# A message-passing layer on one core: the position and flag steps of a block in other iterations, and the variance chain first in its GpSimd queue

## The chip, the cores and the metric

One core of one Trainium2 chip runs the whole layer in one launch. The metric is the time of that launch on the device, in microseconds (us). Engines are named as the profile names them: PE (matmul) and PEld (its weight loads), DVE (VectorE), ACT (ScalarE), POOL (GpSimd), SP (SyncE, which issues the DMAs).

## The reference, cut to what matters

128 graphs of 64 nodes, 128 channels, a 0/1 adjacency with a full diagonal. Each edge gets a message from a three-layer MLP with two layer norms; the messages are summed per node, and a second MLP updates the node.

```python
pair_feats = concatenate([f_i, f_j], axis=-1)          # x of the two ends of each pair
messages = _mlp(pair_feats, msg_w0, msg_b0, ...)       # relu, layernorm, relu, layernorm, linear
messages = messages * coupling_matrix[..., None]       # adj: only edges count
agg = sum(messages, axis=2)
updated = x + _mlp(concatenate([x, agg]), upd_w0, upd_b0, ...)

def _layernorm(x, g, b):
    mu = mean(x); var = mean(square(x - mu))
    return (x - mu) * rsqrt(var + EPS) * g + b
```

## The kernel before, in words

The kernel computes messages for real edges only. The edges of a graph are packed into 640 places, five tiles of 128. Two graphs make a pair `p`, two pairs a quad `q` (20 tiles), and eight graphs (four pairs, two quads) a block `b`. There are 16 blocks, 32 quads, and 160 chunks of four tiles.

**Positions.** For a block, `rank` (DVE scan), `count` (PE), `count_out` and `degrees` (ACT) count edges. `place` (POOL, lines 379, 381, 383) turns the counts into `before`, `mid` and `pos`. `place_out` (line 392, two instructions) masks the positions into `posall`, and `odd_marks` (lines 415, 416) makes `a2`, from which `odd_weights` (DVE) later raises a flag. `distance` (ACT, line 467, tile `d`) reads `mid`; `make_tp` (DVE) makes `tp` from it; `marks` (PE, line 495, tile `mk`) reads `posall` and `tp`. From these come the selectors `s` for layer 0.

**The edge MLP.** One iteration `n` of the main loop handles chunk `n` in layer 0 and chunk `n - 8` in layer 1: `layer1` (PE line 567 and 570 into `z`, ACT line 573 to `y`), `layer0` (PE line 521 into `hps`, ACT line 524 to `h`), `stats0` (PE transposes line 530 into `hT`, DVE line 534 to `st`), `stats1` (DVE line 580 on `y`). PSUM tiles `z`, `hps`, `hT` and `mk` have one buffer each.

**The variance chain.** After the fifth chunk of a quad, `var0_of` (POOL, five small instructions, lines 247 to 251, tile `m`) makes the variance from `st`. In the next iteration `root_of` takes the root on ACT (line 257, `m_sd`), copies it rounded on ACT (line 548), and takes the rest on POOL (line 549, tile `sh`). `turn_root` transposes `sh` on PE (line 554, into `ma`), and ACT copies it to `sdT` (line 559), which layer 1 of that quad reads.

**Other POOL work.** `weights` (line 636, tile `w`, two instructions a pair) scales the one-hot matrices; `var1_step` repeats the variance chain for layer norm 2 (tile `m_v`); per block the node update has `bias0` (lines 683, 686, tile `m`), `residual` (line 690, tile `xo`), `upd_shift` (line 731, tile `usdb`) and two small chains (tile `um`). `reduce` (PE line 651, tile `ys`) sums messages with `w`; `rows` (PE lines 442, 444) makes the next layer-0 tables.

**What sets the order.** The order is written out by hand. `at(n, place, fn, ...)` enters a call into iteration `n` at a place of it; the loop runs the places in a fixed order, and each engine executes its own instructions strictly in that order, waiting on semaphores for others:

```python
run(n, "a"); run(n, "m"); layer1(n - L1); run(n, "b"); layer0(n)
stats0(n - 1); run(n, "k"); stats1(n - L1)
for k in ("x", "x1", "x2", "e1", "e"): run(n, k)
```

Block `b` starts with layer 0 at iteration `o = 10 * b`; quad `q` has its `var0_of` in iteration `5 * q + 5`, entered at "e1", and its `root_of` and `turn_root` one iteration later. `weights` is also at "e1", in iterations 5q + 15 and 5q + 16, and is entered ahead of `var0_of`; nearly all other POOL work is at "e". Below, "iteration 0" to "iteration 9" of a block's period means `n` modulo 10. An odd quad has `var0_of` in iteration 0 and `turn_root` in iteration 1, an even quad in iterations 5 and 6.

Of the kernel before, what the change touches and what calls it, by code (L numbers as in the profile page):

```python
# [23 lines left out]
def tile_gnn(  # L24
# [262 lines left out]
    def edge_path(es):  # L287
# [35 lines left out]
        def at(n, place, fn, *args):  # L323
            plan.setdefault((n, place), []).append((fn, args))

        def run(n, place):
            for fn, args in plan.pop((n, place), ()):
                fn(*args)
# [186 lines left out]
        def layer0(n):  # L515

            ps = ps_h.tile([P, CH * P], F32, name="hps")
            for g, e, c, w in pieces(n):
                s = S[g // 2][:, g % 2, e:e + w]
                for k, ab in enumerate(blocks[g // (2 * PB)]["ab", g // 4 % 2]):  # L520
                    nc.tensor.matmul(ps[:, c:c + w], lhsT=ab[:, g % 4, :], rhs=s,  # L521
                                     start=(k == 0), stop=(k == 1))
            H[n] = hp.tile([P, CH * P], F32, name="h")
            nc.scalar.activation(H[n], ps, AF.Relu, bias=b0c)  # L524

        def stats0(n):
            q, c = divmod(n, QC)
            ps = ps_t.tile([P, CH, P], F32, name="hT")
            for t in range(CH):
                nc.tensor.transpose(ps[:, t, :], H[n][:, t * P:(t + 1) * P], ident)  # L530
            if c == 0:
                ST0[q] = stp.tile([P, QT, 6], F32, name="st0", bufs=2)
            for t in range(CH):
                nc.vector.bn_stats(ST0[q][:, CH * c + t, :], ps[:, t, :])  # L534
# [27 lines left out]
        def layer1(n):  # L562

            q, c = divmod(n, QC)
            ps = ps_z.tile([P, CH, C], F32, name="z")
            h = H.pop(n)
            nc.tensor.matmul(ps, lhsT=SD[q], rhs=W["b1t"][:, CH * c:CH * c + CH, :], start=True,  # L567
                             stop=False, skip_group_check=True)
            for t in range(CH):
                nc.tensor.matmul(ps[:, t, :], lhsT=h[:, t * P:(t + 1) * P], rhs=W["w1c"],  # L570
                                 start=False, stop=True, skip_group_check=True)
            Y[n] = yp.tile([P, CH, C], F32, name="y")
            nc.scalar.activation(Y[n], ps, AF.Relu)  # L573

        def stats1(n):
            q, c = divmod(n, QC)
            if c == 0:
                ST1[q] = stp.tile([P, QT, 6], F32, name="st1", bufs=2)
            for t in range(CH):
                nc.vector.bn_stats(ST1[q][:, CH * c + t, :], Y[n][:, t, :])  # L580
# [122 lines left out]
        def layer(u, *pairs):  # L703
            ps = u.bank()
            for q in range(u.n):
                s = slice(q * P, (q + 1) * P)
                for n, (src, w) in enumerate(pairs):
                    l = (u.blk["xnT"][:, (u.k0 + q) * P:(u.k0 + q + 1) * P] if src == "xn" else
                         getattr(u, src)[:, s])
                    nc.tensor.matmul(ps[:, s], lhsT=l, rhs=w, start=(n == 0),  # L710
                                     stop=(n == len(pairs) - 1))
            u.l_ps = ps[:, 0:u.n * P].rearrange("p (q c) -> p q c", q=u.n)
# [50 lines left out]
        for b in range(NB):  # L763
            o = b * CPB
            if b > 1:
                at(max(o - 25, 0), "a", load_adj, b)
                at(max(o - 12, 0), "a", load_x, b)
            if b > 0:
                r = max(o - 13, 1)
                at(max(o - 14, 0), "m", rank, b)  # L770
                at(r, "x", count, b)
                at(r + 1, "a", count_out, b)
                at(r + 1, "a", degrees, b)
                at(max(o - 11, r + 1), "e", place, b)
                at(max(o - 10, r + 2), "e", place_out, b)
                at(max(o - 10, r + 2), "e", odd_marks, b)
                at(o - 4, "m", odd_weights, b)
                at(o - 3, "x", turn_x, b)
                at(o - 2, "a", turn_x_out, b)
            for half, n in ((0, o - 2), (1, o + 3)):  # L780
                if n >= 0:
                    at(n, "x2", rows, b, half)
                    at(n + 1, "a", rows_hi, b, half)
                    at(n + 1, "m", rows_lo, b, half)

            if b < NB - 2:
                units = [(Unit(b, 0, PB, nc.gpsimd, ubank), o + QC + SC, STEADY)]
            elif b == NB - 2:
                units = [(Unit(b, 0, PB, nc.gpsimd, ubank), o + QC + SC, LAST[0])]
            else:  # L790
                units = [(Unit(b, 0, 2, nc.gpsimd, hbank), o + SC, LAST[1]),
                         (Unit(b, 2, 2, nc.vector, zbank), o + QC + SC - 3, LAST[2])]
            for u, n, t in units:
                at(n - 2, "e", bias0, u)
                at(n + t[0], "a", sums_out, u)
                at(n + t[1], "x", turn, u, "ysum")
                at(n + t[2], "a", turn_out, u, "ysum")
                at(n + t[3], "x", lambda u: layer(u, ("xn", u0a), ("ysumT", W["w2u"])), u)
                at(n + t[4], "m", layer_out, u, "uh", "m0")
                at(n + t[4], "e", upd_m0, u)  # L800
                at(n + t[5], "x", turn, u, "uh")
                at(n + t[6], "a", turn_out, u, "uh")
                at(n + t[7], "a", upd_root0, u)
                at(n + t[7], "e", upd_shift, u)
                at(n + t[8], "x", lambda u: layer(u, ("uhT", W["u1c"])), u)
                at(n + t[8], "e", residual, u)
                at(n + t[9], "m", layer_out, u, "uy", "usdb")
                at(n + t[9], "e", upd_m1, u)
                at(n + t[10], "x", turn, u, "uy")
                at(n + t[11], "a", turn_out, u, "uy")  # L810
                at(n + t[12], "a", upd_root1, u)
                at(n + t[12], "m", upd_inverse, u)
                at(n + t[13], "x", lambda u: layer(u, ("uyT", W["u2c"])), u)
                at(n + t[14], "m", finish, u)
        for p in range(NP):
            n = p * TG * 2 // CH
# [13 lines left out]
            at(NCHK + L1 + 2 if last else p // 2 * QC + SC, "x1", reduce, p)  # L830
        for q in range(NQ):
            n = q * QC + QC
            at(n, "e1", var0_of, q)
            at(n + 1, "b", root_of, q)
            at(n + 1, "x", turn_root, q)
            at(n + 2, "a", root_out, q)
            at(n + L1, "e1", var1_step, q)
            at(n + L1 + (1 if q == NQ - 1 else 2), "a", root1_of, q)
            at(n + L1 + (1 if q == NQ - 1 else 2), "m", inverse_of, q)
# [100 lines left out]
        for n in range(last + 1):  # L940
            run(n, "a")
            run(n, "m")
            if 0 <= n - L1 < NCHK:
                layer1(n - L1)
            run(n, "b")
            if n < NCHK:
                layer0(n)
            if 0 <= n - 1 < NCHK:
                stats0(n - 1)
            run(n, "k")  # L950
            if 0 <= n - L1 < NCHK:
                stats1(n - L1)
            for k in ("x", "x1", "x2", "e1", "e"):
                run(n, k)

        return flag
# [1 line left out]
    with ExitStack() as es:  # L958
        es.enter_context(tc.manual_schedule())
        flag = edge_path(es)  # L960
# [160 lines left out]
```

## Time and profile before

| | us |
|---|---|
| median of 3 runs (lowest, highest) | 650.14 (649.91, 653.18) |
| profiled execution | 653.32 |
| its span, first to last instruction | 651.5 |
| PE busy | 587.4 (90%) |
| DVE busy | 460.8 (71%) |
| ACT busy | 382.5 (59%) |
| POOL busy | 356.4 (55%) |

The span is 1.8 us shorter than the time of its execution. The share of busy time is an average over the span; which engine sets the pace in the loop is read from who waits for whom. A matmul in the profile is pipelined with its neighbours, so that a busy PE is one without gaps. The mean clock granted to TensorE was 0.967 of full speed.

### The profile page before, as it was taken

To read this page: it belongs to the slowest core of one execution; us is meant where nothing else is said; L and a number is where in the kernel's file an instruction comes from. 1 tells how busy PE (TensorE), PEld (TensorE's weight loads), DVE (VectorE), ACT (ScalarE), POOL (GpSimd) and SP (SyncE) were. 2 spreads that over 40 slices of the span, in tenths; PEclk is the share of its full clock that TensorE was granted. 3 is DMA by queue.
4 is the path that set the end of the run, shared out by engine and by line. 5 is a ranking of instruction groups with operands and counts; after the bars stand their busy time and mean duration, and the time that the engine had idled before them with its cause. 6 is when DMAs were issued, how large, how long until landed. Compare 5 with 4: busy or idle time off the path is not lost. (4 is left out here: it accounts for less than half of the span.)

```text
span 651.5 us, 15485 instructions
## 1 busy us (share of the span) xinstructions
PE 587.4 (90%) x5393; PEld 542.0 (83%) x5393; DVE 460.8 (71%) x1868; ACT 382.5 (59%) x781; POOL 356.4 (55%) x919
## 2 busy tenths in 40 slices
PE   5889989898998989899898989999898989998875
PEld 4668879797997979799798979889797979998764
DVE  6666648687676777677687868757786876785674
ACT  5765646665665667475556756655566666663422
POOL 2732355745647574654757465564856556364652
PEclk8998989899999999999999999989999998999998
DMA  4553545345354534625353463444444343431101
GB/s 121 137 139 70 113 93 114 78 112 109 84 127 97 119 88 116 124 64 135 91 130 84 114 122 82 114 108 116 101 114 102 98 104 87 105 95 38 23 17 35
DMA packets 91085, 63.84 MB, mean 98 GB/s; under 512 B 57462, under 2 KB 74876, under 8 KB 91004
## 3 DMA queue, kind: packets, MB, share of 16 engines
q1 hardware_dynamic: 90716, 62.69, 41.3%
q8 instruction: 44, 0.72, 0.5%
q14 instruction: 37, 0.30, 0.1%
q10 hardware_dynamic: 288, 0.13, 0.1%
HBM read 6.82 MB, written 4.19 MB: 17 GB/s over the span
## 5 line engine op out<-in xcount | busy, mean ns | idle before, releaser
L534 DVE BATCH_NORM_STATS2 st<-hT 128x6 f32<-128x128 f32 x640 | 142.3, 285 | 106.8 <-PE hT L530 106.3
L570 PEld LDWEIGHTS z<-w1c,h 128*128 128x128 f32 x1280 | 173.9, 197 | 7.2
L570 PE MATMUL z<-w1c,h 128*128 128x128 f32 x1280 | 174.1, 280 | 0.0
L636 POOL TENSOR_TENSOR w<-oh,m_q 128x320 f32<-128x320 f16 x124 | 86.9, 722 | 152.7 <-PE mk L495 138.2
L573 ACT ACTIVATE y<-z 128x512 f32<-128x512 f32 x160 | 95.5, 597 | 92.1 <-PE z L570 92.1
L580 DVE BATCH_NORM_STATS2 st<-y 128x6 f32<-128x128 f32 x640 | 137.6, 277 | 4.9 <-ACT y L573 4.9
L524 ACT ACTIVATE h<-hps,b0c 128x512 f32<-128x512 f32 x160 | 109.5, 685 | 3.8 <-PE hps L521 3.8
L530 PE MATMUL hT<-ident,h 128*128 128x128 f32 x640 | 98.8, 278 | 0.0
L521 PE MATMUL hps<-s,abl 128*128 128x512 f32 (+3 forms) x256 | 94.6, 380 | 0.4 <-ACT h L524 0.4
L530 PEld LDWEIGHTS hT<-ident,h 128*128 128x128 f32 x640 | 77.7, 143 | 10.0 <-DVE st L534 0.3
L567 PE MATMUL z<-b1t,sdT 80*128 80x512 f32 x160 | 80.5, 503 | 1.6 <-ACT y L573 1.6
L521 PE MATMUL hps<-s,abh 128*128 128x512 f32 (+3 forms) x256 | 80.5, 332 | 0.0
L651 PE MATMUL ys<-y,w 128*64 128x128 f32 x1280 | 78.2, 278 | 0.0
L651 PEld LDWEIGHTS ys<-y,w 128*64 128x64 f32 x1280 | 70.5, 139 | 7.3 <-issue 7.0
L503 DVE TENSOR_TENSOR j<-mk,cmpt 128x320 fp32r<-128x320 f32 x126 | 59.7, 473 | 1.5 <-PE mk L495 1.4
L458 DVE TENSOR_TENSOR abl<-mu,abh 128x512 fp32r<-128x512 f32 x32 | 22.1, 690 | 50.2 <-ACT abh L451 50.2
L467 ACT ACTIVATE d<-slot,mid 128x640 f16<-128x640 f16 x64 | 53.4, 834 | 0.0
L521 PEld LDWEIGHTS hps<-s,abl 128*128 128x128 f32 x256 | 51.4, 201 | 1.7 <-ACT i L479 0.8
L521 PEld LDWEIGHTS hps<-s,abh 128*128 128x128 f32 x256 | 51.4, 201 | 0.0
L451 ACT CAST abh<-mu 128x512 fp32r<-128x512 f32 x32 | 18.7, 585 | 48.3 <-PE mu L444 48.3
L479 ACT CAST i<-tp 128x640 fp32r<-128x640 f16 x63 | 45.4, 720 | 1.9 <-DVE tp L473 1.9
L554 PE MATMUL ma<-ident,sh 128*80 128x128 f32 x32 | 10.0, 312 | 38.2 <-POOL sh L549 38.1
(221 smaller groups left out, 1000.1 us busy)
## 6 DMA issues: line engine op xcount, KB each, us to landing
s<-i SPq DMA_DIRECT2D x126, 160.0 KB, 2.7
s<-j SPq DMA_DIRECT2D x126, 160.0 KB, 2.6
xn<-in_x_dram SPq DMA_DIRECT2D x15, 256.0 KB, 3.8
out_dram<-uo SPq DMA_DIRECT2D x15, 256.0 KB, 2.4
an<-in_adj_dram SPq DMA_DIRECT2D x16, 128.0 KB, 2.7
oh<-tp SPq DMA_TRANSPOSE x64, 2.6
xn<-in_x_dram SPq DMA_DIRECT2D x2, 128.0 KB
out_dram<-uo SPq DMA_DIRECT2D x2, 128.0 KB
```

The source lines that it names most:

```text
L467: nc.scalar.activation(D[p], slot, AF.Abs, bias=blocks[b]["mid"][:, q:q + 1], scale=-1.0)
L503: nc.vector.tensor_tensor(JR[p][:, c], MK.pop((p, k))[:, 0:HC], cmpt[:, c], op=ALU.is_equal)
L521: nc.tensor.matmul(ps[:, c:c + w], lhsT=ab[:, g % 4, :], rhs=s, start=(k == 0), stop=(k == 1))
L524: nc.scalar.activation(H[n], ps, AF.Relu, bias=b0c)
L530: nc.tensor.transpose(ps[:, t, :], H[n][:, t * P:(t + 1) * P], ident)
L534: nc.vector.bn_stats(ST0[q][:, CH * c + t, :], ps[:, t, :])
L567: nc.tensor.matmul(ps, lhsT=SD[q], rhs=W["b1t"][:, CH * c:CH * c + CH, :], start=True, stop=False, skip_group_check=True)
L570: nc.tensor.matmul(ps[:, t, :], lhsT=h[:, t * P:(t + 1) * P], rhs=W["w1c"], start=False, stop=True, skip_group_check=True)
L573: nc.scalar.activation(Y[n], ps, AF.Relu)
L580: nc.vector.bn_stats(ST1[q][:, CH * c + t, :], Y[n][:, t, :])
L636: (nc.vector if p // 2 == NQ - 1 else nc.gpsimd).tensor_tensor(w[:, :, g, :], OH[p][:, :, g * N:(g + 1) * N], Q[q][:, k:k + TG].unsqueeze( ...
L651: nc.tensor.matmul(YS[b][g * N:(g + 1) * N, k, :], lhsT=w[:, t, g, :], rhs=y, start=(t == 0), stop=(t == TG - 1))
```

## The change

Two edits. In every block from the third on (`b` = 2 to 15), `place` moves from iteration `o - 11` to `o - 9`, and `place_out` with `odd_marks` from `o - 10` to `o - 7`, all still at place "e", behind whatever that iteration has entered before. And `var0_of` gets a place "e0" of its own, run ahead of "e1", so that it stands ahead of `weights`.

```diff
-                at(max(o - 11, r + 1), "e", place, b)
-                at(max(o - 10, r + 2), "e", place_out, b)
-                at(max(o - 10, r + 2), "e", odd_marks, b)
+                at(max(o - 9, r + 1), "e", place, b)
+                at(max(o - 7, r + 2), "e", place_out, b)
+                at(max(o - 7, r + 2), "e", odd_marks, b)
...
-            at(n, "e1", var0_of, q)
+            at(n, "e0", var0_of, q)
...
-            for k in ("x", "x1", "x2", "e1", "e"):
+            for k in ("x", "x1", "x2", "e0", "e1", "e"):
```

No instruction is added or removed. Only POOL's queue changes its order: PE, DVE, ACT and SP have the same rows in the same order as before, with other buffer numbers. On POOL there are three places, shown for one period in the middle of the program.

POOL before, from iteration 9 to iteration 1 of a period (odd quad): the last two rows of `place`, then `weights`, the five variance instructions, `place_out`, `odd_marks`, and only then `sh`.

```order
L381 TENSOR_TENSOR mid<-cumall,before 128x4
L383 TENSOR_TENSOR pos<-rk,before 128x256
L636 TENSOR_TENSOR w<-oh,m_q 128x5x64 x2
L247 TENSOR_TENSOR m_d<-st_4047 128x20
L248 TENSOR_TENSOR m_s<-st_4047 128x20
L249 TENSOR_TENSOR m_d<-m_d 128x20
L250 TENSOR_SCALAR m_d<-m_d 128x20
L251 TENSOR_TENSOR m_4325<-m_d,m_s 128x20
L392 TENSOR_TENSOR posall<-pos,an 64x4x64 x2
L415 TENSOR_TENSOR a_4333<-an 128x256
L416 TENSOR_TENSOR a_4333<-a_4333,an 128x256
L549 TENSOR_TENSOR sh<-m_sd,sh 128x40
```

Of these rows, the first two and those of lines 392 to 416 move to later iterations, and the `w` pair moves behind line 251.

POOL after, iterations 0 and 1 of the same period: the variance instructions first, then `weights` of the first pair, then `sh`; behind `sh` the second pair's `weights`, `residual`, `bias0`, and now `place`.

```order
L247 TENSOR_TENSOR m_d<-st_4047 128x20
L248 TENSOR_TENSOR m_s<-st_4047 128x20
L249 TENSOR_TENSOR m_d<-m_d 128x20
L250 TENSOR_SCALAR m_d<-m_d 128x20
L251 TENSOR_TENSOR m_4316<-m_d,m_s 128x20
L636 TENSOR_TENSOR w<-oh,m_q 128x5x64 x2
L549 TENSOR_TENSOR sh<-m_sd,sh 128x40
L636 TENSOR_TENSOR w<-oh,m_q 128x5x64 x2
L690 TENSOR_TENSOR xo<-xn,cu2b 128x512
L683 TENSOR_TENSOR m_4381<-c2u,deg 128x512
L686 TENSOR_TENSOR m_4381<-m_4381,ub0b 128x512
L379 TENSOR_TENSOR before<-cumall,deg 128x4
```

So four instructions left the stretch between `m` and `sh`, one pair of `w` entered it, and `place` went from an idle stretch to the end of iteration 1's queue.

POOL after, iteration 3 to iteration 5 of that period: `place_out` and `odd_marks` now follow the layer norm 2 chain (`m_v`), ahead of the even quad's variance chain. Before, line 265 was followed there by `w`.

```order
L265 TENSOR_TENSOR m_v<-m_v,m_4516 128x20
L392 TENSOR_TENSOR posall<-pos,an 64x4x64 x2
L415 TENSOR_TENSOR a_4525<-an 128x256
L416 TENSOR_TENSOR a_4525<-a_4525,an 128x256
L247 TENSOR_TENSOR m_d<-st_4357 128x20
```

What moved there: the two steps that stood ahead of `sh` stand two iterations behind it.

## The prediction

> **What bounds the kernel now.** I read the page first, then the list of who waits for whom, then the order of time around the largest wait. From the page: the span, TensorE's busy share, and the granted clock in 40 slices. From the list of waits, TensorE's two largest.
>
> ```profile
> span 651.5 us, 15485 instructions
> PE 587.4 (90%) x5393; PEld 542.0 (83%) x5393; DVE 460.8 (71%) x1868; ACT 382.5 (59%) x781; POOL 356.4 (55%) x919
> PEclk8998989899999999999999999989999998999998
> ...
> PE ma L554 <- POOL sh L549: 38.1, 17, 3.3
> PE mk L495 <- DVE tp L473: 4.9, 3, 3.5
> ```
>
> PE is idle for 651.5 - 587.4 = 64.1 us, and 38.1 us of that is one wait: the transpose of `sh` (line 554) for POOL. It occurs 17 times. The next wait is an eighth of it. Three of the 17 stand outside the places that the change touches; these are their rows in order of time.
>
> ```profile
> 30.33 0.31 PE L554 MATMUL ma<-ident,sh 128*80 128x128 f32 x1 [1.87 <-POOL sh L549]
> ...
> 65.86 0.31 PE L554 MATMUL ma<-ident,sh 128*80 128x128 f32 x1 [0.34 <-POOL sh L549]
> ...
> 607.80 0.31 PE L554 MATMUL ma<-ident,sh 128*80 128x128 f32 x1 [0.98 <-POOL sh L549]
> ```
>
> The other 14 hold 38.1 - 1.87 - 0.34 - 0.98 = 34.9 us. They are the odd quads of blocks 2 to 15, one per block; no even quad of the steady loop is in the list. Here is one of them in order of time (start, duration, engine, line; in brackets the idle time before it and what ended it).
>
> ```profile
> 381.63 0.89 DVE L534 BATCH_NORM_STATS2 st<-hT 128x6 f32<-128x128 f32 x4
> 381.81 1.40 POOL L636 TENSOR_TENSOR w<-oh,m_q 128x320 f32<-128x320 f16 x2 [5.29 <-PE mk L495]
> 383.17 0.25 POOL L247 TENSOR_TENSOR m_d<-st 128x20 f32<-128x20 f32 x1
> 384.22 0.23 POOL L251 TENSOR_TENSOR m<-m_d,m_s 128x20 f32<-128x20 f32 x1
> 384.40 1.52 POOL L392 TENSOR_TENSOR posall<-pos,an 64x256 f16<-64x256 f32 x2
> 384.48 0.31 ACT L257 ACTIVATE m_sd<-m,eps_c 128x20 f32<-128x20 f32 x1 [0.54 <-POOL m L251]
> 384.82 0.23 ACT L548 CAST sh<-m_sd 128x40 fp32r<-128x40 f32 x1
> 386.00 0.61 POOL L415 TENSOR_TENSOR a<-an 128x256 f32<-128x256 f32 x1
> 386.69 0.72 POOL L416 TENSOR_TENSOR a<-a,an 128x256 f32<-128x256 f32 x1
> 387.38 0.27 POOL L549 TENSOR_TENSOR sh<-m_sd,sh 128x40 fp32r<-128x40 f32 x1
> 387.70 0.31 PE L554 MATMUL ma<-ident,sh 128*80 128x128 f32 x1 [2.35 <-POOL sh L549]
> ```
>
> ACT has delivered the rounded root at 384.82 + 0.23 = 385.05, but POOL is in `place_out` and `odd_marks` until 387.41. PE has been ready since 387.70 - 2.35 = 385.35. A second loss ahead of it: the statistics are complete at 381.63 + 0.89 = 382.52, and the chain starts at 383.17, when `w` is done.
>
> **The stall also costs clock.** The first two rows are whole periods of a block between two such transposes, the others stretches right at or after one (columns: stretch, its length, busy time by engine, granted clock, DMA).
>
> ```profile
> 387.70:424.70 37.00, 34.66 (x334) 32.49 (x334) 27.83 (x114) 23.28 (x47) 21.98 (x58) 1.00 0.44 108
> 424.70:463.30 38.60, 36.24 (x334) 34.01 (x334) 27.72 (x114) 23.38 (x47) 21.97 (x58) 0.96 0.42 103
> ...
> 45.90:52.70 6.80, 5.94 (x24) 4.92 (x24) 0.92 (x4) 2.59 (x6) 1.06 (x3) 0.50 0.50 121
> 537.40:540.60 3.20, 3.19 (x14) 3.10 (x15) 0.28 (x2) 0.85 (x2) 3.20 (x4) 0.50 0.88 197
> ```
>
> A full-clock period has 37.00 - 34.66 = 2.34 us of PE idle time, which is the stall and nothing else: PE sets the pace, and every microsecond of the stall that goes shortens the span. After seven of the 14 stalls the clock is at half for some 3.4 us (after the first, at 46.76, for 6.8 us; those two rows are the first and the last of the seven). Such a period lasts 38.60 instead of 37.00 us. In the PEclk line five of the seven drops show as an 8 (two are split between slices); the first and the last 8 are the program's ends.
>
> **The change, part by part.** *Variance chain first.* Between engines a hand-over takes about 0.05 (`sh` ends at 387.38 + 0.27 = 387.65, PE starts at 387.70); I allow 0.08, so POOL can start `m_d` at 382.60 instead of 383.17. The five instructions take 384.45 - 383.17 = 1.28, so `m` is ready at 383.88. ACT then delivers its copy within the 0.60 it now needs (385.05 - 384.45), at about 384.5.
>
> *place_out and odd_marks out.* They held 387.41 - 384.40 = 3.0 us between `m` and `sh`. The pair `w` with 1.40 takes their place: from 383.84 to 385.24. Its inputs were there at 381.81, 2 us earlier, so it does not wait. `sh` starts at 385.20 instead of 387.38, and PE at 385.52 instead of 387.70. **Gain 2.18 us**, with 0.17 of stall left. Times 14: 30.5 us. The bounds are 34.9 (all of the stall) and, if `w` ran 0.5 slower in its new place, 23.5. I take 30.5, since the durations are those of the same instructions.
>
> *Even quads.* There `sh` now stands behind `w`: 1.40 behind `m` instead of some 0.6, with `m` 0.57 earlier; 0.2 us later in all. No even quad has PE waiting, and the nearest bound is the odd quad's 0.17 left over: 0, at worst 14 x 0.2 = 3.
>
> *place moved behind the queue of iteration 1.* Before, it ran in POOL's idle time in iteration 9; the rows of its duration come first. Now it follows `sh`, `w`, `xo` and `m` (`bias0`), and ACT's `d` in iteration 3 needs its `mid`. All these rows are of before:
>
> ```profile
> 375.48 0.20 POOL L379 TENSOR_TENSOR before<-cumall,deg 128x4 f32<-128x4 f32 x1
> 375.75 0.20 POOL L381 TENSOR_TENSOR mid<-cumall,before 128x4 f32<-128x4 f32 x1
> ...
> 387.61 1.40 POOL L636 TENSOR_TENSOR w<-oh,m_q 128x320 f32<-128x320 f16 x2
> 388.96 1.29 POOL L690 TENSOR_TENSOR xo<-xn,cu2b 128x512 f32<-128x512 f32 x1
> 390.21 1.04 POOL L683 TENSOR_TENSOR m<-c2u,deg 128x512 f32<-128x512 f32 x1
> 390.23 0.83 ACT L467 ACTIVATE d<-slot,mid 128x640 f16<-128x640 f16 x1
> 391.33 1.28 POOL L686 TENSOR_TENSOR m<-m,ub0b 128x512 f32<-128x512 f32 x1
> 391.33 0.60 ACT L573 ACTIVATE y<-z 128x512 f32<-128x512 f32 x1 [0.28 <-PE z L570]
> 391.87 0.69 ACT L524 ACTIVATE h<-hps,b0c 128x512 f32<-128x512 f32 x1
> 392.35 2.40 PE L651 MATMUL ys<-y,w 128*64 128x128 f32 x40
> 392.69 0.22 POOL L263 TENSOR_SCALAR um_v<-um 128x4 f32<-128x4 f32 x1
> 395.56 0.50 PE L567 MATMUL z<-b1t,sdT 80*128 80x512 f32 x1
> 395.94 0.23 POOL L265 TENSOR_TENSOR m_v<-m_v,m 128x20 f32<-128x20 f32 x1
> 396.71 0.48 PE L521 MATMUL hps<-s,abl 128*128 128x512 f32 x1
> ```
>
> In these rows' clock (subtract 2.18 for the new one): `m` ends at 392.61, so `mid` is ready at 392.69 + 0.47 = 393.16, while `d` would start at 390.23. ACT waits 2.9 us, in twelve blocks (4 to 15; in block 3, where `xo` is missing, 1.3 us less). Behind `d` in ACT's queue stand `y` and `h` of iteration 3; they end at 393.2 + 0.83 + 0.60 + 0.6 = 394.6 for `y` and 395.3 for `h`. Who needs them? PE's next `z` needs the bank that `y` reads, but PE is first in `reduce` (2.40 us) and `rows`, and comes to `z` at 395.56: 0.9 later. Its next `hps` is at 396.71: 1.4 after `h`. So the wait is covered by `reduce` and `rows`; cost 0, and up to 2.9 x 12 + 1.6 = 36 us if the cover were gone.
>
> *place_out two iterations later.* POOL's small chains (`um` and `m_v`) run from 392.69 to 396.17, now some 1.1 later because of `place` ahead: to 397.3. `place_out` ends at 398.8, `odd_marks` at 400.2. Their readers, still in that clock:
>
> ```profile
> 399.79 0.30 PE L495 MATMUL mk<-tp,posall 128*128 128x320 f16 x1
> 399.99 0.89 DVE L534 BATCH_NORM_STATS2 st<-hT 128x6 f32<-128x128 f32 x4
> ```
>
> `mk` reads `posall` 1.0 us after it is written, and the even quad's statistics are complete at 400.88, 0.7 after POOL comes free. Cost 0, with thin margins: each microsecond of POOL beyond them would show as 14 us.
>
> *Clock.* If the stalls go, so should the drops. Seven drops, eight stretches of 3.4 us (the first counts twice), each worth 38.60 - 37.00 = 1.6 us: 12.8. Bounds 0, and 8 x 3.4 / 2 = 13.6. I take 12.8, because no full-clock period in the trace shows a drop elsewhere.
>
> In a sentence of its own, a rule that speaks against this term: the Trainium skill, page "TensorE: Matmul & The Clock Gate", section "HAM oscillation", says that PE-idle gaps of over about 3.4 us bring the clock down. No stall here exceeds 3.3 us, so by that rule the drops would have another cause and stay, and the sum would be 12.8 us smaller. The trace disagrees in so far as the half-clock rows above start at such stalls.
>
> **Sum.** 30.5 + 12.8 = 43.3 us off the profiled execution of 653.3 (span 651.5 and 1.8 around it): 610 us. The median of the runs before is 3.2 lower than that execution; I don't take that off, as the sum removes the whole term that may differ between executions, the drops.
>
> **The rivals.**
> - *The drops stay*, whatever the stall does. For it: the other half of the stalls has none. Against: all seven sit at a stall. 653.3 - 30.5 = 623. Chance 0.08.
> - *Part of the slack is used up*: `mk` waits for `posall`, or POOL is late for the even quad, by 1 to 2 us in each block, most likely where POOL and DVE slow each other. 610 + 14 to 28 = 624 to 638. For it: margins of 0.7 and 1.0. Against: every duration is from the same loop. Chance 0.08.
> - *Slower: the wait of `d` for `mid` reaches PE.* Its place is ACT's queue in iteration 3, its price up to 2.9 us in twelve blocks. It decides when `mid` is later than PE's cover: from 0.9 us more delay on it costs PE, and at 0.9 + 2.2 more it takes all of the stall gain. If the cover isn't there at all, PE's stalls add up to 36 us against 30.5, and they are long enough to keep the drops: 653.3 - 30.5 + 36 = 659. Against: `reduce` and `rows` stand in PE's order ahead of that `z`, 3.4 us of work. Chance 0.04.
> - *The change doesn't do what it says*, since `w` ahead of `sh` waits for its own inputs as long as `place_out` took. Against: at 381.81 they were there. 650. Chance 0.02.
>
> **The numbers.** My forecast of 610 has 0.78. The range reaches from 603 (all of the 34.9 and 13.6 gone is 653.3 - 48.5 = 604.8, less 2 for executions that differ) to 628, which takes in the drops that stay and the lighter half of the used-up slack; some 0.88 of the chance. Faster by over 0.5% (about what a measurement here can tell from no change) are the forecast, the first two rivals and whatever is left unnamed between them: 0.94. Within 0.5%: 0.02. Slower: 0.04.
>
> **What would show it.** Right: PE's wait for `sh` at some 14 x 0.17 + 3.2 = 6 us in place of 38.1; a period of about 34.8 us; PE near 96% busy; the granted clock at 0.99, with drops at the two ends only; a new wait of ACT's `d` for POOL's `mid` of about 3 us in twelve blocks, with no wait of PE on `y` behind it. Wrong: PE waiting on line 567 for `y`, on line 495 for `posall`, or half-clock stretches in the middle of the loop without a stall before them.

## The result and the profile after

The changed kernel takes 614.92 us (median of 4 runs, 614.85 to 615.34), the kernel before 651.66 us beside it: a ratio of 0.9434, 95% interval 0.9394 to 0.9474. It is faster, as forecast; 614.9 lies inside 603 to 628 and 4.9 us above 610. The profiled execution took 615.34 us with a span of 613.6: 38.0 us off the 653.32 of before, where the sum had 43.3.

The page of the changed kernel, the same three lines as were shown of the kernel before:

```profile
span 613.6 us, 15457 instructions
PE 577.3 (94%) x5393; PEld 532.1 (87%) x5393; DVE 478.1 (78%) x1868; ACT 379.1 (62%) x781; POOL 361.7 (59%) x919
PEclk9999999999999999999999999999999999999987
```

The work of every engine has the same counts as before; the 28 instructions that the page has less are semaphore instructions, 27 on DVE and one on POOL. All the 8s in the loop are gone; what is left is at the end of the program. From the list of waits (engine and line, who ended it, us in total, times, longest):

```profile
POOL m_d L247 <- DVE st L534: 131.1, 31, 8.8
...
ACT d L467 <- POOL mid L381: 34.2, 13, 2.7
...
PE ma L554 <- POOL sh L549: 10.6, 18, 1.9
...
PE mk L495 <- DVE tp L473: 4.6, 2, 3.4
```

PE's wait for `sh` fell from 38.1 to 10.6 us. POOL's idle time now ends with DVE's statistics: the chain no longer queues behind `w`. ACT waits for `mid`, which it did not before, and no wait of PE on `y` or `posall` has come up. The same place of the program as was shown of before, in order of time:

```profile
356.54 0.89 DVE L534 BATCH_NORM_STATS2 st<-hT 128x6 f32<-128x128 f32 x4
357.51 0.25 POOL L247 TENSOR_TENSOR m_d<-st 128x20 f32<-128x20 f32 x1 [7.10 <-DVE st L534]
358.52 0.37 DVE L473 TENSOR_SCALAR tp<-d,deg 128x640 f16<-128x640 f16 x1
358.57 0.40 POOL L251 TENSOR_TENSOR m<-m_d,m_s 128x20 f32<-128x20 f32 x1
358.93 1.40 POOL L636 TENSOR_TENSOR w<-oh,m_q 128x320 f32<-128x320 f16 x2
359.35 0.22 ACT L548 CAST sh<-m_sd 128x40 fp32r<-128x40 f32 x1
...
360.29 0.27 POOL L549 TENSOR_TENSOR sh<-m_sd,sh 128x40 fp32r<-128x40 f32 x1
360.61 0.31 PE L554 MATMUL ma<-ident,sh 128*80 128x128 f32 x1 [0.37 <-POOL sh L549]
```

The chain starts 0.08 after the statistics (356.54 + 0.89 = 357.43). But line 251 takes 0.40 where it took 0.23, while DVE's `tp` runs at the same time. And ACT has its copy ready at 359.57, while POOL is in `w` until 360.33: what PE still waits for is `w`.

### The profile page after: what moved, and what is told of

It is laid out like the page before. It is cut to its first block, busy times and chain, and to the rows that moved or that the text cites. A ratio compares the mean times of both kernels' runs of the same rounds, so it can differ in the third digit from the quotient of the medians.

```text
span 613.6 us, 15457 instructions
## 1 busy us (share of the span) xinstructions
PE 577.3 (94%) x5393; PEld 532.1 (87%) x5393; DVE 478.1 (78%) x1868; ACT 379.1 (62%) x781; POOL 361.7 (59%) x919
## 5 line engine op out<-in xcount | busy, mean ns | idle before, releaser
L570 PEld LDWEIGHTS z<-w1c,h 128*128 128x128 f32 x1280 | 168.3, 192 | 6.9
L570 PE MATMUL z<-w1c,h 128*128 128x128 f32 x1280 | 168.8, 275 | 0.0
L247 POOL TENSOR_TENSOR m_d<-st 128x20 f32<-128x20 f32 x62 | 15.5, 250 | 146.7 <-DVE st L534 131.1
L530 PE MATMUL hT<-ident,h 128*128 128x128 f32 x640 | 97.2, 275 | 0.0
L636 POOL TENSOR_TENSOR w<-oh,m_q 128x320 f32<-128x320 f16 x124 | 91.8, 761 | 5.8 <-PE hT L530 5.0
L521 PE MATMUL hps<-s,abl 128*128 128x512 f32 (+3 forms) x256 | 92.1, 372 | 0.4 <-ACT h L524 0.4
L567 PE MATMUL z<-b1t,sdT 80*128 80x512 f32 x160 | 78.4, 490 | 1.6 <-ACT y L573 1.6
L521 PE MATMUL hps<-s,abh 128*128 128x512 f32 (+3 forms) x256 | 78.3, 324 | 0.0
L521 PEld LDWEIGHTS hps<-s,abl 128*128 128x128 f32 x256 | 49.5, 193 | 1.8 <-ACT i L479 0.9
L521 PEld LDWEIGHTS hps<-s,abh 128*128 128x128 f32 x256 | 49.5, 193 | 0.0
```

What stands on the lines that cost most here:

```text
L636: (nc.vector if p // 2 == NQ - 1 else nc.gpsimd).tensor_tensor(w[:, :, g, :], OH[p][:, :, g * N:(g + 1) * N], Q[q][:, k:k + TG].unsqueeze( ...
```

## The experiments

Each ratio below is against runs of the kernel before on the same chip. The three groups of runs were on three chips, on which the kernel before took 653.48, 654.63 and 653.29 us, so that medians of different groups compare to about 1 us. The order of POOL between the statistics and `sh` can be set with one edit or the other, the stall can be given back in doses, and `mid` can be made later. The changed kernel ran again beside the first three.

**The changed kernel again.**

> The changed kernel again, on the chip of the three runs beside it, as their reference. 614 to 616 us; the profiled run loses the loop's half-clock stretches as before. If the missing clock drops were luck of where the 3.4 us stretches fall, some run of it shows one and 1.6 us more.

616.84 us (615.23 to 618.33), ratio 0.9446 (0.9415 to 0.9477), 0.8 us above what was expected. Its profile, of the fastest run, has no half-clock stretch in the loop either. The two slowest of its six runs, 617.78 and 618.33 us, have a mean granted clock of 0.980 and 0.979 where the others have 0.991 to 0.993. So those two probably had further half-clock stretches; without a profile of them it is open where.

**The second edit alone.**

```diff
-            at(n, "e1", var0_of, q)
+            at(n, "e0", var0_of, q)
-            for k in ("x", "x1", "x2", "e1", "e"):
+            for k in ("x", "x1", "x2", "e0", "e1", "e"):
```

> Only the second edit: the variance chain ahead of the weights, with place, place_out and odd_marks where they were. My theory, that the stall is the POOL work between the variance m and sh: the pair w now also stands there (1.40 us), the chain starts only some 0.57 earlier, so sh comes 0.8 us later than before in 14 blocks: 12 us slower than the kernel before, 662, and the stall of PE grows from 2.35 to about 3.2. Rival, that starting the chain earlier is what gained: a gain of up to 0.57 x 14 = 8 us, 643.

690.62 us, ratio 1.0555 (1.0508 to 1.0601): slower than before by 37 us, three times what I expected. The queue is as foretold. Four views of it: rows in order of time, the page's clock line, PE's largest wait, and one period of a block.

```profile
367.11 0.40 POOL L251 TENSOR_TENSOR m<-m_d,m_s 128x20 f32<-128x20 f32 x1
367.47 1.40 POOL L636 TENSOR_TENSOR w<-oh,m_q 128x320 f32<-128x320 f16 x2
...
368.83 1.52 POOL L392 TENSOR_TENSOR posall<-pos,an 64x256 f16<-64x256 f32 x2
...
371.80 0.27 POOL L549 TENSOR_TENSOR sh<-m_sd,sh 128x40 fp32r<-128x40 f32 x1
...
372.13 0.43 PE L554 MATMUL ma<-ident,sh 128*80 128x128 f32 x1 [3.35 <-POOL sh L549]
```

```profile
PEclk9989989998998989899898998999999898999997
```

```profile
PE ma L554 <- POOL sh L549: 51.6, 18, 4.2
```

```profile
331.20:372.10 40.90, 37.57 (x334) 35.24 (x334) 28.53 (x113) 23.29 (x47) 22.41 (x58) 0.92 0.44 97
```

The stall is 3.35 us, and all its waits together are 51.6 - 38.1 = 13.5 us longer than before. That is my 12. The other 25.7 of the 39.2 us of span (690.7 - 651.5) are clock: this whole period is granted 0.92, and PE is busy for 37.57 us of it where a full-clock period has 34.66. The theory of where the stall comes from stands, the rival falls, and my price for a stall was wrong: a longer one costs clock out of proportion.

**The first edit alone.**

```diff
-                at(max(o - 11, r + 1), "e", place, b)
-                at(max(o - 10, r + 2), "e", place_out, b)
-                at(max(o - 10, r + 2), "e", odd_marks, b)
+                at(max(o - 9, r + 1), "e", place, b)
+                at(max(o - 7, r + 2), "e", place_out, b)
+                at(max(o - 7, r + 2), "e", odd_marks, b)
```

> Only the first edit: place, place_out and odd_marks moved, weights ahead of the chain as before. My theory: m some 0.5 us later than in the changed kernel, but no w between m and sh, so sh starts when ACT's rounded root is there; stall 0.1 to 0.25 us instead of 0.38, and 2 to 4 us faster than the changed kernel: 611 to 613. Rival, that the chain's place carries part of the gain: 0.57 x 14 = 8 us slower than the changed kernel, 623.

610.65 us, ratio 0.9353 (0.9321 to 0.9384), 6.2 us faster than the changed kernel beside it, where 2 to 4 were expected (the profiled spans differ by 613.4 - 608.7 = 4.7); again in a later run 610.61, ratio 0.9342 (0.9316 to 0.9368). From its profile, in three views: PE's wait, the same place in order of time, and a period (stretch, length, busy time of PE, PEld, DVE, ACT, POOL, clock, DMA):

```profile
PE ma L554 <- POOL sh L549: 4.9, 5, 1.9
```

```profile
356.12 0.23 POOL L251 TENSOR_TENSOR m<-m_d,m_s 128x20 f32<-128x20 f32 x1
...
356.72 0.22 ACT L548 CAST sh<-m_sd 128x40 fp32r<-128x40 f32 x1
357.02 0.27 POOL L549 TENSOR_TENSOR sh<-m_sd,sh 128x40 fp32r<-128x40 f32 x1 [0.68 <-ACT sh L548]
357.34 0.12 PEld L554 LDWEIGHTS ma<-ident,sh 128*80 128x80 f32 x1 [0.30 <-POOL sh L549]
```

```profile
357.30:392.10 34.80, 34.66 (x334) 32.49 (x334) 28.07 (x114) 23.04 (x48) 22.34 (x58) 1.00 0.47 115
```

`sh` follows ACT's copy at once. The chain ends later than in the changed kernel and still almost in time: PE is busy for 34.66 of 34.80 us, and its stall is 0.11. So the second edit, which the change makes as well, costs it some 6 us. With it, `w` stands between `m` and `sh`; the last experiment takes `w` out of there with the chain still first.

**place left where it was.**

```diff
-                at(max(o - 10, r + 2), "e", place_out, b)
-                at(max(o - 10, r + 2), "e", odd_marks, b)
+                at(max(o - 7, r + 2), "e", place_out, b)
+                at(max(o - 7, r + 2), "e", odd_marks, b)
```

> Only place_out and odd_marks moved; place stays in iteration o - 11, where POOL is idle, and the chain stays behind the weights. My theory: ACT's wait of d for mid (34 us in the changed kernel) is gone, and it is worth nothing, as PE's work covers it: within 1 us of the run with both moves. Rival, that this wait costs PE something: faster than that run by several us.

612.62 us, ratio 0.9390 (0.9358 to 0.9421): 2 us above the run with both moves where 1 was expected at most; the intervals overlap. Its list of waits has no line of ACT's `d` for `mid`. PE's wait is

```profile
PE ma L554 <- POOL sh L549: 5.5, 6, 1.9
```

as short as with both moves. So 34 us of waiting on ACT is worth nothing measurable, and the gain belongs to `place_out` and `odd_marks` alone.

**The stall given back in doses.** To the changed kernel, one, two or three idle POOL products are added behind the variance chain of the odd quads (in the loop of `var0_of`; the count is 1, 2 or 3):

```diff
             V0[q] = square_sum(stp, ST0.pop(q), QT, "m20", eng_of(q))
+            if q % 2 and q < NQ - 4:
+                for i in range(3):
+                    nc.gpsimd.tensor_tensor(idle, first, first, op=ALU.mult)
```

> The changed kernel with one idle POOL product (128x256, about 0.61 us and 0.08 to the next) behind the variance chain of the 14 odd quads, ahead of w and sh; its result is used nowhere. PE's stall grows from 0.38 to about 1.1 us: 14 x 0.69 = 10 us more, 625. By the theory that the clock drops come from stalls of this length or longer only, none yet. If any stall costs clock, 625 plus up to 12.

> Two such products: stall about 1.8 us, 14 x 1.38 = 19 us over the changed kernel, 635 without clock drops. Stalls of 2.35 had 7 drops in 14 and stalls of 3.35 had 14, most of them doubled, so I expect few here, 0 to 4: 635 to 641. By the page's rule of idle gaps of over 3.4 us (the Trainium skill, "TensorE: Matmul & The Clock Gate"): none, 635.

> Three such products: stall about 2.45 us, as before the change: 14 x 2.07 = 29 us over the changed kernel, 645, and by the theory that the stall itself brings the drops some 7 to 9 half-clock stretches of 3.4 us at 1.6 each come back: 656 to 660, slower than the kernel before by 3 to 6. Rival, that the drops belonged to the old order and not to the stall, or need 3.4 us of idle time: 645.

| | stall in the steady loop, us | median, us | ratio (interval) |
|---|---|---|---|
| changed kernel | 0.37 | 616.84 | 0.9446 (0.9415 to 0.9477) |
| one | 0.94 | 624.24 | 0.9527 (0.9509 to 0.9545) |
| two | 1.61 | 634.65 | 0.9688 (0.9671 to 0.9705) |
| three | 2.33 | 653.53 | 0.9988 (0.9959 to 1.0016) |

The clock lines of one, two and three doses, each from its page:

```profile
PEclk9999999999999999999999999999999999998998
```

```profile
PEclk9998989999999999999999999999999999999998
```

```profile
PEclk8999989899998999999899999989999999999998
```

PE's waits for `sh` in all, with one, two and three doses:

```profile
PE ma L558 <- POOL sh L553: 18.0, 18, 1.9
```

```profile
PE ma L558 <- POOL sh L553: 27.3, 18, 2.5
```

```profile
PE ma L558 <- POOL sh L553: 37.2, 18, 3.2
```

One and two doses cost 7 and 18 us over the changed kernel, about what the stall lengthens (18.0 - 10.6 = 7.4 and 27.3 - 10.6 = 16.7). The third costs 19 more, with 9.9 us of stall in it. With it the 8s are back in the middle of the loop, and the kernel takes the time of the kernel before. Its profile has six half-clock stretches in the loop where 7 to 9 were expected, and its median is 2.5 us below the range expected. With two doses, two stretches came, both in the early blocks: one after the stall of 2.53 us shown below, one after a stall of only 1.20 us at 46.63. In order of time, with two doses: the largest stall there and one of the steady loop, and the clock of the stretch around the first and of the steady period ahead of the second:

```profile
84.52 0.31 PE L558 MATMUL ma<-ident,sh 128*80 128x128 f32 x1 [2.53 <-POOL sh L553]
...
375.11 0.31 PE L558 MATMUL ma<-ident,sh 128*80 128x128 f32 x1 [1.61 <-POOL sh L553]
```

```profile
82.00:89.00 7.00, 4.48 (x23) 4.28 (x24) 3.06 (x14) 3.32 (x7) 6.77 (x12) 0.76 0.49 117
...
338.80:375.10 36.30, 34.68 (x334) 32.50 (x334) 29.07 (x114) 23.02 (x47) 23.63 (x60) 1.00 0.49 110
```

(Line 554 is 558 here.) So the stall itself brings the drops: with nothing else of the old order, 2.33 us of it restores the old time. Against the rule of about 3.4 us of idle time (the Trainium skill, "TensorE: Matmul & The Clock Gate", section "HAM oscillation") the trace decides: gaps of 2.3 to 2.5 us suffice some of the time.

Why only some of the time can be read from the clock records. In every trace of this case the half-clock stretches begin and end on a grid of 3.41 us. What comes before a drop in the loop, with one exception, is a step of this grid in which PE is idle for more than half. Two stalls of the kernel before, and the steps of the grid around them (stretch, length, PE, PEld, DVE, ACT, POOL, clock, DMA):

```profile
274.62 0.44 PE L554 MATMUL ma<-ident,sh 128*80 128x128 f32 x1 [2.35 <-POOL sh L549]
...
313.64 0.31 PE L554 MATMUL ma<-ident,sh 128*80 128x128 f32 x1 [2.83 <-POOL sh L549]
```

```profile
271.13:274.54 3.41, 1.13 (x10) 0.94 (x8) 3.16 (x13) 1.74 (x4) 3.17 (x7) 1.00 0.22 50
274.54:277.95 3.41, 3.33 (x15) 3.24 (x16) 0.36 (x2) 0.86 (x2) 3.41 (x5) 0.50 0.84 192
...
308.67:312.09 3.42, 2.15 (x19) 1.91 (x17) 2.99 (x14) 2.23 (x5) 3.10 (x9) 1.00 0.02 5
312.09:315.50 3.41, 1.85 (x16) 1.82 (x17) 1.33 (x5) 0.76 (x3) 3.33 (x6) 1.00 0.92 226
```

The first stall lies almost whole in one step, which is left with 3.41 - 1.13 = 2.28 us idle, and the next step is at half clock. The second is longer, but it is split between two steps with 1.27 and 1.56 us idle, and no drop follows. Counted over the twelve traces between 40 and 580 us, all 30 full-clock steps with 1.88 us or more of idle PE are followed by a half-clock step. Of the 1813 with 1.87 us or less, one is: that of the 1.20 us stall above, which stays unexplained. No run moved a stall along the grid on purpose, so this is a reading of the traces and not a test; and in the tail of the program, where the work is another, steps with 1.64 to 1.74 us idle are followed by a drop too.

**mid later still.**

```diff
-                at(max(o - 9, r + 1), "e", place, b)
+                at(max(o - 8, r + 1), "e", place, b)
```

> The changed kernel with place one iteration later still (o - 8), where it stands behind the um chain, so mid is some 1.6 us later. Theory of the cover: in the changed kernel y of iteration 3 ends 1.2 us before PE needs its bank, so mid 1.6 later makes PE's z wait for y by about 0.45 us in 12 blocks: 5 us slower than the changed kernel, and ACT waits for mid by about 4.3 us each. Rival, that d is not on any path to PE: no change. Other rival, that the cover was thinner than I read: 1.6 x 12 = 19 us slower.

624.53 us, ratio 0.9550 (0.9524 to 0.9575): 7.7 us above the changed kernel's median, 5 expected. In order of time, and a period:

```profile
371.51 0.83 ACT L467 ACTIVATE d<-slot,mid 128x640 f16<-128x640 f16 x1 [4.36 <-POOL mid L381]
372.25 0.58 ACT L573 ACTIVATE y<-z 128x512 f32<-128x512 f32 x1
...
372.88 0.51 PE L567 MATMUL z<-b1t,sdT 80*128 80x512 f32 x1 [0.44 <-ACT y L573]
```

```profile
364.50:400.20 35.70, 34.88 (x335) 32.49 (x336) 28.43 (x114) 22.96 (x48) 22.46 (x58) 1.00 0.46 112
```

ACT waits 4.36 us instead of 2.72, and now PE waits 0.44 for `y`, just where the prediction's rival had put it. The period is longer by 35.70 - 35.05 = 0.65, of which 0.44 is this wait; 0.2 shows as a longer busy PE (34.88 instead of 34.66; more on it in the next experiment). In twelve blocks 0.65 makes 7.8 us, which is the cost measured. So `d` is on a path to PE, and the cover of `reduce` and `rows` is real and thin: with 1.64 us more the wait has outrun it.

**A version with nothing between.** `place` in its idle stretch, `place_out` and `odd_marks` moved, the chain first, and the first pair's weights one iteration later:

```diff
-            at(NCHK + L1 + 1 if last else w + 2, "e1", weights, p)
+            at(NCHK + L1 + 1 if last else w + 3 - p % 2, "e1", weights, p)
```

> place_out and odd_marks moved as in the change, place left in its idle stretch (o - 11), the variance chain first, and the weights of the first pair one iteration later, so that nothing stands between m and sh and nothing ahead of the chain. My theory: in the steady loop PE has no stall on sh, as with the moves alone, so an earlier sh buys nothing there; only the early quads' 0.3 to 1.0 us shrink: 0 to 2 us faster than the moves alone, 609 to 611. Rival, that an earlier chain still pays: 0.5 x 14 = 7 us faster, 604.

> The moves alone again, as the reference of the run beside it: 609 to 612.

608.46 us, ratio 0.9318 (0.9284 to 0.9353), beside 610.61 for the moves alone. Both beat the changed kernel; the 2 us between them are within the intervals. PE's wait for `sh`, and a period of the steady loop:

```profile
PE ma L554 <- POOL sh L549: 4.5, 5, 1.9
```

```profile
337.16:371.62 34.46, 34.46 (x336) 32.45 (x335) 27.68 (x114) 22.96 (x47) 22.07 (x58) 1.00 0.54 116
```

So the chain ahead of the weights costs nothing when `w` does not stand behind `m`. It even gains a little: with the moves alone each period still had a stall of 0.11 us and lasted some 34.8 us, and here PE has no gap at all. In the profiles that is 3.7 us over the twelve steady blocks, of which some 1.6 are lost again at the end of the program, where PE once waits 2.07 us for `y` (0.72 with the moves alone). The busy time of PE tells a second thing: a period has 34.46 us of it without a gap, 34.66 or 34.67 with one gap, be it 0.11 or 2.35 us long, and 34.88 with the two gaps of `mid later still`. So in these periods each gap of PE cost some 0.2 us beside its own length.

## Why the prediction was right, and where its sizes were off

**The stall, 30.5 us forecast, 27.5 measured** (38.1 - 10.6). The mechanism and the place were right: `place_out` and `odd_marks` ahead of `sh`. The stalls are those that the prediction meant, but they belong to the odd quads of blocks 0 to 13; what it called blocks 2 to 15 are the blocks whose `place_out` stands there. The mis-sized step is the 1.28 us for the five small instructions and so the 0.17 of stall left. It is 0.38, for line 251 takes 0.40 instead of 0.23 when DVE's `tp` runs beside it; the chain had been moved under that instruction. In twelve blocks that is 12 x 0.2 = 2.4 us. The rest is the even quad at 63.66, which the step on even quads had at 0 and whose wait is now 0.97 instead of 0.34; `sh` stands behind `w` there, which takes 1.78 us instead of 1.40:

```profile
63.66 0.31 PE L554 MATMUL ma<-ident,sh 128*80 128x128 f32 x1 [0.97 <-POOL sh L549]
```

**A step that failed in its reading.** The prediction counted the chain's earlier start as a second loss to be won back. The runs with one edit alone show that it is none: ahead of the weights the chain costs 37 us without the moves (two thirds of it clock), and 6 us with them, since what it wins before `m` is less than the `w` that it brings behind `m`.

**The clock, 12.8 us forecast.** From the first transpose of `sh` to the end, the span shortened by (651.5 - 30.33) - (613.6 - 31.81) = 39.4 us; without the 27.5 of the stall, 11.9 is left for the clock. PE's busy time over the same stretch agrees: 567.8 us before, 556.0 after. The term was right, and that the stalls bring the drops is now shown by the doses and not only argued. What the prediction left open, that half of the stalls had none, goes in the traces by where a stall falls on the grid of 3.41 us. The other 1.5 us of the gap to 43.3 lie ahead of that transpose:

```profile
31.81 0.31 PE L554 MATMUL ma<-ident,sh 128*80 128x128 f32 x1 [1.86 <-POOL sh L549]
```

It stood at 30.33 in the one trace of the kernel before and stands at 31.2 to 32.1 in all the others. The rows of work up to there are the same before and after; the same 119 matmuls were busy for 19.53 us before and 21.31 after. So it is no effect of the new order; what made them slower is not shown.

**The new wait.** ACT waits for `mid` 2.72 us in twelve blocks and 1.49 in one; the working had 2.9 and 1.6. It is hidden where the prediction put it. (Its sum for the end of `y` is written with one 0.6 too many: 393.2 + 0.83 + 0.60 is the 394.6 that it goes on with.) These rows are of the changed kernel, in order of time:

```profile
365.99 0.83 ACT L467 ACTIVATE d<-slot,mid 128x640 f16<-128x640 f16 x1 [2.73 <-POOL mid L381]
...
366.73 0.58 ACT L573 ACTIVATE y<-z 128x512 f32<-128x512 f32 x1
...
368.48 0.50 PE L567 MATMUL z<-b1t,sdT 80*128 80x512 f32 x1
...
370.03 1.53 POOL L392 TENSOR_TENSOR posall<-pos,an 64x256 f16<-64x256 f32 x2
...
372.70 0.30 PE L495 MATMUL mk<-tp,posall 128*128 128x320 f16 x1
...
373.87 0.25 POOL L247 TENSOR_TENSOR m_d<-st 128x20 f32<-128x20 f32 x1 [0.81 <-DVE st L534]
```

`y` is done 1.2 us before PE's `z` (0.9 forecast), `posall` 1.1 before `mk` (1.0), and POOL is free 0.8 before the even quad's statistics (0.7). The thin margins held as worked out from the rows of before.

**The marks it set.** PE's wait 10.6 us (6 foretold; the prediction's own sum leaves 38.1 - 30.5 = 7.6, since three of the 14 stalls were longer than 2.4), a period of 35.05 (34.8), PE busy 94% (96), clock 0.992 (0.99).

## What to carry to other kernels

On an in-order engine, look at what stands between the two halves of a chain whose other half is elsewhere, not only at what stands ahead of its first half: emptying the gap between `m` and `sh` gained nearly all, and starting the chain earlier cost time wherever it put `w` into that gap. Price a wait by the work that stands in the waiting engines' queues behind it: 34 us of ACT waiting cost nothing here, and 1.6 us more of it in each block began to cost. And a repeated gap of TensorE can cost more than its length, so read the clock rows before you put a price on a stall.

## What was not expected

- The price of a stall in clock rises steeply: in the steady loop no half-clock stretch with 0.37, 0.94 or 1.61 us, one behind 10 of the 23 stalls of 2.3 to 2.4, and one behind each of the twelve of 3.35, nine of them 6.8 us long. The kernel with the second edit alone lost twice as much by it as by its longer stall.
- POOL and DVE instructions can take longer side by side. Line 251 took 0.40 to 0.42 us in most places with DVE's `tp` beside it and 0.22 to 0.23 wherever `tp` was not; `tp` itself took 0.84 beside POOL's `posall` and 0.37 beside line 251. It was seen in the rows of several kernels and not tested by a run of its own.
